# Both banks of a PSUM pair in turns for the early experts, an even pace for the threshold search, and a residual moved into the second attention

## The chip, the cores and the metric

The kernel runs on one core of a Trainium2 chip. The metric is the device time of one execution in microseconds (us). Times are the median of timed executions; beside them stands one execution taken with the hardware profiler, whose own time is given with its span.

## The reference

Sixteen batches of 256 tokens with 128 channels pass through four residual steps in fp32. The experts' step is used twice with the same weights.

```
x = x + attn_a(layernorm(x))      # 16 heads of 8 channels, sign-and-scale weights
x = x + ffn(layernorm(x))
x = x + attn_b(layernorm(x))      # 16 heads, with a table of relative positions
x = x + ffn(layernorm(x))

def ffn(x):                       # 8 experts of 512 hidden units, every token in every expert
    logits = einsum('bld,ed->ble', x, gate_weight)
    kth    = sort(logits.reshape(-1))[4 * 128 * 6 - 1]   # one threshold for all tokens
    gates  = logits * (logits >= kth)
    h      = gelu(einsum('bld,ehd->bleh', x, w1) + b1)
    y      = einsum('bleh,edh->blde', h, w2) + b2
    return einsum('blde,ble->bld', y, gates)
```

The threshold is one order statistic of all logits of the step. It is known only when the attention before it has finished its last batch, while the hidden layers of the experts need only the tokens of their own chunk.

## The kernel before

**Stages.** The order is the first attention, the first experts, the second attention, the second experts. A chunk is 512 tokens (two batches); there are 8 chunks (`NCHUNK`) and 8 experts (`NE`), so 64 pairs of chunk and expert per pass. For one pair `h_unit` (L1082) is one matmul of 128x512 into a PSUM tile `ph` and one gelu on ScalarE (ACT) into `hT`, four times; `y_unit` (L1093) is four matmuls of 128x512 into one tile `py`. One fp32 matmul is two records in the trace.

**Early experts.** The first two chunks (`EARLY` = 16 pairs of chunk and expert) do not wait for the threshold: `early` (L1102) is a generator that yields after each h unit and after each y unit, 80 pieces in all, and the y results go ungated to `raw` tiles by an ACT activation (L1116). Twenty pieces are taken at the end of the attention before (`own_at`, L1054, by the step `U` of the second attention: 20 pieces), the rest during the search.

**PSUM at the end of the second attention.** The scores of the second attention use three PSUM tiles with the tag `ss` of two banks each (L875). The early pieces there take tiles of the same tag through `bank` (L1074) and use the first bank of each, `[:, 0, :]`; a tile comes free for the next piece but two when ACT has read it. Two more banks have the tag `m`. All engines are written out by hand there (`manual_schedule`, L1009), so each queue runs in the order of the code: PE has, for steps `U` = 128 and on, the visits `first` and `second` of the last batches and between them the pieces.

**The search.** `search` (L1144) finds the threshold bit by bit in 11 counts. A count compares all logits with up to seven candidates on VectorE (DVE, lines L1137), sums over the partitions by a small matmul `pc` (L1141), and four small DVE operations choose the next candidates. `experts` (L1249) takes four early pieces for each of the 11 counts; where `pc` stands among them on PE is decided by the scheduler. After it the gates are turned by `pg` (L1259), written to DRAM, and read back as rows `gb` for each pair (L1189, seven buffers).

**The border from the first experts to the second attention.** The last pair of chunk and expert is done in halves of 256 tokens: `last_in_halves` (L1215) makes two `py` of four 128x256 matmuls each; each half is gated on DVE (L1225), added to the sum `acc` (L1228), transposed by two PE matmuls `f_pr` (L1236), and added to `x` (L1239). Then the second attention begins with its first matmuls L726 (queries of batch 1), whose PSUM bank belonged to the experts' pool, and the scores L884.

Of the kernel before, what the change touches and what calls it, by code (L numbers as in the profile page):

```python
# [10 lines left out]
F32 = mybir.dt.float32  # L11
I32 = mybir.dt.int32
AF = mybir.ActivationFunctionType
ALU = mybir.AluOpType
# [64 lines left out]
def hybrid_kernel(ctx: ExitStack, tc: tile.TileContext, io):  # L79
# [38 lines left out]
    def const(name):  # L118
        lo, hi = CONSTS[name]
        return head[:, lo:hi]  # L120
# [532 lines left out]
    def attention_b(outer):  # L653
# [35 lines left out]
        def values_tile(pool, i):  # L689

            va = pool.tile([P, NK, NJ, DH, NG], F32, tag=f"va{i}", name=f"b_va{i}")
            nc.gpsimd.memset(va, 0.0)
            vas.append(va)

        values_tile(wpool, 0)
        mask_h, mask_q = const("mask_h"), const("mask_q")
        NH2, NN = NH // 2, NQB // 2
        rows_of, xnTs, batch, vz, tall = {}, {}, {}, {}, {}
# [160 lines left out]
        def main(st, place, filling):  # L859
# [176 lines left out]
            def for_batch(f, b, *rest):  # L1036
# [13 lines left out]
                6: lambda b: for_batch(ahead_rows, b + 3),  # L1050
                7: lambda b: for_batch(ahead_spread, b + 1),
            }

            own_at = {0: 2, 1: 2, 2: 1, 4: 2, 5: 2, 6: 2, 8: 2, 9: 2, 10: 1, 12: 2, 13: 2}  # L1054
            done = 0
            for U in range(total + 2 * NU + 1):
                b, i = divmod(U, NU)
                table.get(i, lambda b: None)(b)
                if U < total:
                    scores(U)  # L1060
                while done < min(total, U - 1):
                    turn(done)
                    done += 1
                if U >= total:
                    place["h"] = (epool, 5, psum, "ss", 3)
                    place["y"] = (psum, "ss", 3)
                    place["raw"] = (epool, 4)
                    for _ in range(own_at.get(U - total, 0)):
                        own.append(next(filling))

        return begin, run


    def bank(psum, tag, name, bufs):  # L1074

        if callable(tag):
            return tag(name).rearrange("p t x -> p (t x)")
        if tag == "ss":
            return psum.tile([P, 2, CH], F32, tag=tag, name=name, bufs=bufs)[:, 0, :]
        return psum.tile([P, CH], F32, tag=tag, name=name, bufs=bufs)  # L1080

    def h_unit(place, c, e, k):  # L1082
# [37 lines left out]
                    yield  # L1120
            prev = (c, e, hs)

    def experts(last, place, raw, filling, middle):
        with ExitStack() as st:
            hpool = st.enter_context(tc.tile_pool(name="f_h", bufs=1))
            pool = st.enter_context(tc.tile_pool(name="f_2", bufs=2))
# [3 lines left out]

            def count(thresholds, name):

                n = len(thresholds)
                cnt = small.tile([P, NCAND], F32, tag="cnt", name=f"cnt{name}")
                for j, threshold in enumerate(thresholds):
                    ge = small.tile([P, NTILE * NE], F32, tag="ge", name=f"ge{name}_{j}", bufs=2)
                    nc.vector.tensor_scalar(  # L1137
                        ge, lf, threshold, 0.0, ALU.is_ge, ALU.add, accum_out=cnt[:, j : j + 1]
                    )
                pc = psum.tile([P, NCAND], F32, tag="c", name=f"pc{name}")  # L1140
                nc.tensor.matmul(pc[:, 0:n], ones, cnt[:, 0:n], start=True, stop=True)  # L1141
                return pc

            def search():  # L1144

                digits = const("digits")

                pc = count((0.0, 2.0, -2.0 + 2.0**-23), "s")  # L1150
                ok = small.tile([P, 3], F32, tag="ok_s", name="ok_s")
                held = small.tile([P, 1], F32, tag="held", name="held_s")
                nc.vector.tensor_scalar(
                    ok, pc[:, 0:3], NEED, 0.0, ALU.is_ge, ALU.add, accum_out=held
                )
                below = small.tile([P, 1], I32, tag="d", name="below")
                nc.vector.tensor_scalar(below, held, 2.0, -1.0, ALU.is_lt, ALU.mult)
                f = below
                for odd in (1.0, 3.0):
                    d = small.tile([P, 1], I32, tag="d", name=f"d_s{odd:.0f}")  # L1160
                    nc.vector.tensor_scalar(
                        d, held, odd, float(1 << 30), ALU.is_equal, ALU.mult
                    )
                    new = small.tile([P, 1], I32, tag="f", name=f"f_s{odd:.0f}")
                    nc.vector.tensor_tensor(new, f, d, ALU.bitwise_xor)
                    f = new
                yield
                for i in range(len(SHIFTS)):
                    at = slice(NCAND * i, NCAND * i + NCAND)
                    cand = small.tile([P, NCAND], I32, tag="cand", name=f"cand{i}")  # L1170
                    nc.vector.tensor_tensor(  # L1171
                        cand, flips[:, at], f.to_broadcast([P, NCAND]), ALU.bitwise_xor
                    )
                    values = cand.bitcast(F32)
                    pc = count([values[:, j : j + 1] for j in range(NCAND)], i)
                    ok = small.tile([P, NCAND], F32, tag="ok", name=f"ok{i}")
                    nc.vector.scalar_tensor_tensor(  # L1177
                        ok, pc, NEED, digits[:, at], ALU.is_ge, ALU.mult
                    )
                    d = small.tile([P, 1], I32, tag="d", name=f"d{i}")  # L1180
                    nc.vector.tensor_reduce(d, ok, AX.X, ALU.max)  # L1181
                    new = small.tile([P, 1], I32, tag="f", name=f"f{i}")
                    nc.vector.tensor_tensor(new, f, d, ALU.bitwise_xor)  # L1183
                    f = new
                    yield
                kth.append(f)

            def broadcast_gates(c, e):
                gb = pool.tile([P, CH], F32, tag="gb", name=f"gb{c}_{e}", bufs=7)  # L1189
                nc.sync.dma_start(  # L1190
                    gb.rearrange("p (t k) -> p t k", k=P),
                    gd[c * 4 * NE : (c + 1) * 4 * NE, :]
                    .rearrange("(t e) k -> e t k", e=NE)[e]
                    .partition_broadcast(P),
                )
                return gb
# [3 lines left out]
            def gated(c, e, y, bias):  # L1200

                gb = broadcast_gates(c, e)
                if e == 0:
                    accs[c] = pool.tile([P, CH], F32, tag="acc", name=f"acc{c}", bufs=2)
                    dst = accs[c]
                else:
                    dst = pool.tile([P, CH], F32, tag="gy", name=f"gy{c}_{e}")
                if bias is None:
                    nc.vector.tensor_tensor(dst, y, gb, ALU.mult)
                else:  # L1210
                    nc.vector.scalar_tensor_tensor(dst, y, bias, gb, ALU.add, ALU.mult)  # L1211
                if e:
                    nc.vector.tensor_tensor(accs[c], accs[c], dst, ALU.add)
# [32 lines left out]
            place["h"] = (hpool, 14, psum, "h", 3)  # L1246
            place["y"] = (psum, "y", 2)
            place["raw"] = (pool, EARLY - 4)
            for i, _ in enumerate(search()):  # L1249
                for _ in range(4):  # L1250
                    next(filling, None)
            gates = small.tile([P, NTILE * NE], F32, tag="ge", name="gates", bufs=2)
            nc.vector.scalar_tensor_tensor(
                gates, lf, kth[0].bitcast(F32), lf, ALU.is_ge, ALU.mult
# [13 lines left out]
            for i in range(EARLY, total + 1):  # L1268
                c, e = divmod(i, NE)
                hs, now, ready = None, ready, []  # L1270
                if i < total:
                    hs = [h_unit(place, c, e, k) for k in range(NHC)]
                if middle is not None and i >= total - 12 and i % 2 == 0:
                    next(middle(psum), None)
                if due < EARLY:
                    gated(*divmod(due, NE), raw[due], None)
                    due += 1
                    if due % NE == 0:
                        ready.append(due // NE - 1)
                if i == total:  # L1280
                    last_in_halves(*prev)
                elif prev is not None:
                    gated(
                        prev[0], prev[1], y_unit(place, *prev),
                        b2[:, prev[1] : prev[1] + 1],
                    )
                    if prev[1] == NE - 1:
                        ready.append(prev[0])
                for done in now:
                    residual(done)  # L1290
                prev = (c, e, hs)
            for done in ready:
                residual(done)

    epool = ctx.enter_context(tc.tile_pool(name="epool", bufs=1))
# [6 lines left out]
    ahead = fill()  # L1302
    attention_a(*ahead[::2])
    with ExitStack() as st:
        begin, run = attention_b(st)
        experts(False, *ahead, begin)
        ahead = fill()
        run(*ahead[::2])
    experts(True, *ahead, None)


def _spread(v, extra):
# [73 lines left out]
```

## Time and profile before

| | |
|---|---|
| timed runs | 1535.77, 1535.91 and 1536.73 us, median 1535.91 |
| profiled execution, own time | 1538.61 us |
| its span, first to last instruction | 1536.6 us |
| granted TensorE clock over the span | 0.999 |
| PE busy | 1523.6 us (99%), 12292 matmul records |
| ACT, DVE, POOL busy | 839.5, 799.5 and 406.4 us |
| second attention | about 740 to 1079 us of the span |
| early pieces at its end | 1078.8 to 1108.7 us |
| second search, from its first to its last `pc` | 1110.9 to 1168.3 us |

Times in views of the trace are microseconds from the start of the span. The row of a group gives busy time, mean duration and the idle time of its engine before it, with what ended that idle time. PE matmuls are pipelined and their ends are modelled, so the start of one record against the start of the next tells more of PE than the length of one.

### The profile page before, as it was taken

What the parts mean: (1) busy time and instruction counts of PE and PEld (TensorE: products, weight loads), DVE (VectorE), ACT (ScalarE), POOL (GpSimd) and SP (SyncE); (2) the same over time, 40 slices, a digit from 0 to 9 for tenths busy, and PEclk for the clock granted to TensorE, in tenths of its full rate; (3) what the DMA queues carried; (4) which work ended last, traced back from release to release, by engine and by line L of the source; (5) the groups of instructions that cost most, each with busy time, mean ns of one, the idle gap of its engine ahead of it and who ended that gap; (6) DMA issues with size and microseconds to landing.
All of it is one profiled execution on the core that took longest, in us unless ns stands there. A gap on an engine that the chain in (4) does not pass through costs nothing. (4 is left out here: it accounts for less than half of the span.)

```text
span 1536.6 us, 30874 instructions
## 1 busy us (share of the span) xinstructions
PE 1523.6 (99%) x12292; PEld 858.9 (56%) x12292; DVE 799.5 (52%) x1624; ACT 839.5 (55%) x2092; POOL 406.4 (26%) x521
## 2 busy tenths in 40 slices
PE   9999999999999999999999999999999999999998
PEld 6777777544444444444677777777444444444444
DVE  7878887254134221212699999999353143212222
ACT  4666666644434343434688888888544433434342
POOL 6323421200001000002488988886100000000000
PEclk9999999999999999999999999999999999999999
DMA  4511110000223211120122222221002133111110
GB/s 107 149 30 36 37 29 16 5 4 9 71 75 78 53 37 39 38 46 20 27 53 58 50 51 48 54 57 37 8 1 63 43 81 85 50 46 39 44 41 7
DMA packets 174127, 69.91 MB, mean 45 GB/s; under 512 B 74520, under 2 KB 173600, under 8 KB 173728
## 3 DMA queue, kind: packets, MB, share of 16 engines
q1 hardware_dynamic: 173408, 67.54, 18.7%
q8 instruction: 97, 1.59, 0.4%
q10 hardware_dynamic: 576, 0.41, 0.1%
q14 instruction: 46, 0.38, 0.1%
HBM read 50.88 MB, written 12.58 MB: 41 GB/s over the span
## 5 line engine op out<-in xcount | busy, mean ns | idle before, releaser
L1088 ACT ACTIVATE hT<-ph,head 128x512 f32<-128x512 f32 x512 | 351.1, 687 | 419.2 <-PE ph L1086 416.7
L1086 PE MATMUL ph<-xn,w 128*128 128x512 f32 x1024 | 464.3, 594 | 1.1 <-ACT hT L1088 1.1
L1097 PE MATMUL py<-hT,w 128*128 128x512 f32 (+1 forms) x1040 | 461.1, 586 | 1.0 <-ACT logits L985 0.5
L1097 PEld LDWEIGHTS py<-hT,w 128*128 128x128 f32 x1040 | 196.6, 190 | 237.3 <-issue 230.5
L1086 PEld LDWEIGHTS ph<-xn,w 128*128 128x128 f32 x1024 | 191.4, 190 | 228.5 <-issue 224.7
L1211 DVE SCALAR_TENSOR_TENSOR gy<-py,head,gb 128x512 f32<-128x512 f32 x82 | 61.5, 750 | 425.7 <-PE py L1097 425.7
L899 ACT ACTIVATE b_pr<-b_s,b_nm 128x256 f32<-128x256 f32 x512 | 235.9, 473 | 61.2 <-DVE b_nm L894 60.9
L455 DVE TENSOR_REDUCE a_nm<-a_s 128x2 f32<-128x512 f32 x256 | 158.5, 682 | 50.7 <-PE a_t L478 49.0
L894 DVE TENSOR_REDUCE b_nm<-b_s 128x4 f32<-128x1024 f32 x128 | 152.7, 1193 | 23.8 <-PE b_s L884 23.6
L884 PE MATMUL b_s<-b_kT,b_qd 64*64 64x256 f32 x1024 | 160.8, 384 | 0.0
L884 PE MATMUL b_s<-strip,b_qb 64*64 64x256 f32 x2048 | 157.6, 378 | 0.0
L884 PE MATMUL b_s<-b_kS,b_qd 64*64 64x256 f32 x1024 | 157.4, 384 | 0.0
L909 DVE STREAM_TRANSPOSE b_pT<-b_pr 128x1024 f32<-128x1024 f32 x128 | 157.1, 1228 | 0.0
L484 ACT ACTIVATE a_pT<-a_t 128x512 f32<-128x512 f32 x256 | 132.6, 602 | 29.2 <-PE a_t L478 28.8
L478 PE MATMUL a_t<-a_qa,a_qk 32*128 32x256 f32 x1024 | 133.8, 392 | 0.1
L774 POOL TENSOR_TENSOR b_qd<-b_qsel,head 128x512 f32<-128x512 f32 x64 | 84.1, 1335 | 179.8 <-DMA b_qsel<-b_qT 169.5
L450 PE MATMUL a_s<-a_qk 32*128 32x256 f32 x1024 | 128.4, 389 | 0.3 <-ACT a_qkc L416 0.3
L153 POOL TENSOR_SCALAR ve<-mv 128x2 f32<-128x2 f32 x64 | 14.8, 231 | 423.4 <-DVE mv L150 413.6
L450 PEld LDWEIGHTS a_s<-a_qk 32*128 32x128 f32 x1024 | 91.6, 184 | 22.6 <-issue 14.9
L899 ACT ACTIVATION_READ_ACCUMULATOR b_pr<-b_s,b_nm 128x1 f32 x512 | 104.1, 203 | 0.0
L478 PEld LDWEIGHTS a_t<-a_qa,a_qk 32*128 32x128 f32 x1024 | 99.7, 184 | 3.9 <-PE a_t L478 0.8
L162 POOL TENSOR_SCALAR xn<-x,mv,rstd 128x128 f32<-128x128 f32 x126 | 99.9, 803 | 6.6
(175 smaller groups left out, 1432.8 us busy)
## 6 DMA issues: line engine op xcount, KB each, us to landing
gb<-gd SPq DMA_DIRECT2D x128, 256.0 KB
w<-in_w SPq DMA_DIRECT2D x2, 2048.0 KB
a_qks<-a_qkc SPq DMA_DIRECT2D x15, 256.0 KB
a_qk<-a_qks SPq DMA_DIRECT2D x60, 64.0 KB
x<-in_x SPq DMA_DIRECT2D x16, 128.0 KB
b_qs<-b_qT SPq DMA_DIRECT2D x64, 32.0 KB
b_qsel<-b_qT SPq DMA_DIRECT2D x64, 32.0 KB
b_z<-b_qs SPq DMA_DIRECT2D x16, 128.0 KB
```

The source lines that it names most:

```text
L162: (last or nc.gpsimd).tensor_scalar(xn[:, t, :], xs[b][:, t, :], mv[:, t, 0:1], rstd[:, t : t + 1], ALU.subtract, ALU.mult,)
L450: nc.tensor.matmul(sc[:, t, :], q[b][rows, g, t * P : (t + 1) * P], k[b][rows, g, :], start=True, stop=True,)
L455: nc.vector.tensor_reduce(nms[G % 4][:, :, j, 0:1].rearrange("p t o -> p (t o)"), sc, AX.X, ALU.max, negate=True,)
L478: nc.tensor.matmul(sc[:, t, :], k[b][rows, g, t * P : (t + 1) * P], qaug[G][rows, :], start=True, stop=True,)
L484: nc.scalar.activation(pT, sc, AF.Exp)
L884: nc.tensor.matmul(sc[64 * c : 64 * c + 64, r, u, :], (qb_[rows, at, c] if rel else qd[rows, at, x]).rearrange("p h q -> p (h q)"), strip[ ...
L894: nc.vector.tensor_reduce(nm, sc, AX.X, ALU.max, negate=True)
L899: nc.scalar.activation(pr[:, u, r, :], sc[:, r, u, :], AF.Exp, bias=nm[:, r, u : u + 1], scale=1.0, accum_out=sums[b][:, n : n + 1],)
L909: nc.vector.transpose(pT[:, half % 2, 4 * i : 4 * i + 4].rearrange("p n k h q -> p (n k h q)"), probs.pop(U).rearrange("p u r k -> p (u r ...
L1086: nc.tensor.matmul(ph, w1[:, m * P : (m + 1) * P], xn2[c], start=True, stop=True)
L1088: nc.scalar.activation(hT, ph, AF.Gelu_apprx_tanh, bias=b1[:, m : m + 1], scale=1.0)
L1097: nc.tensor.matmul(py[:, 0:width], w2[:, e * NHC + k, :], hs[k], start=k == 0, stop=k == NHC - 1)
```

## The change

It has three parts. At the end of the second attention `bank` hands out both banks of an `ss` tile in turns, first bank and then second bank, before it takes a new tile. In the search the small matmul of a count stands after five early pieces, in an order on PE that is written by hand, and the yield stands between the comparisons and that matmul. For the first experts the last pair is no longer done in halves: its sum goes to a tile `late` in the attention's pool, and the transposes and the additions to `x` of chunk 7 are done by `add_late` in step `U` = 2 of the second attention. To make room `gb` has six buffers instead of seven in the first experts.

```diff
+        late = wpool.tile([P, CH], F32, tag="late", name="b_late_sum")
...
+            def add_late():
+                pr = psum.tile([P, 2 * T], F32, tag="m", name="b_late", bufs=2)
+                for t in range(4):
+                    nc.tensor.transpose(
+                        pr[:, t * P : (t + 1) * P], late[:, t * P : (t + 1) * P], ident
+                    )
+                for j in range(2):
+                    b = NB - 2 + j
+                    nc.vector.tensor_tensor(
+                        xs[b], xs[b],
+                        pr[:, j * T : (j + 1) * T].rearrange("p (t c) -> p t c", c=C), ALU.add,
+                    )
...
                 table.get(i, lambda b: None)(b)
+                if U == 2:
+                    add_late()
                 if U < total:
                     scores(U)
...
+    halves = []
     def bank(psum, tag, name, bufs):
...
         if tag == "ss":
-            return psum.tile([P, 2, CH], F32, tag=tag, name=name, bufs=bufs)[:, 0, :]
+            if not halves:
+                t = psum.tile([P, 2, CH], F32, tag=tag, name=name, bufs=bufs)
+                halves.extend((t[:, 1, :], t[:, 0, :]))
+            return halves.pop()
...
             def count(thresholds, name):
...
                         ge, lf, threshold, 0.0, ALU.is_ge, ALU.add, accum_out=cnt[:, j : j + 1]
                     )
+                yield
                 pc = psum.tile([P, NCAND], F32, tag="c", name=f"pc{name}")
...
-                    pc = count([values[:, j : j + 1] for j in range(NCAND)], i)
+                    pc = yield from count([values[:, j : j + 1] for j in range(NCAND)], i)
...
-                    yield
                 kth.append(f)
...
-                gb = pool.tile([P, CH], F32, tag="gb", name=f"gb{c}_{e}", bufs=7)
+                gb = pool.tile([P, CH], F32, tag="gb", name=f"gb{c}_{e}", bufs=7 if last else 6)
...
                 if e == 0:
-                    accs[c] = pool.tile([P, CH], F32, tag="acc", name=f"acc{c}", bufs=2)
+                    if c == NCHUNK - 1 and not last:
+                        accs[c] = late
+                    else:
+                        accs[c] = pool.tile([P, CH], F32, tag="acc", name=f"acc{c}", bufs=2)
...
-            for i, _ in enumerate(search()):
-                for _ in range(4):
-                    next(filling, None)
+            with tc.manual_schedule(engines={mybir.EngineType.PE}):
+                for _ in search():
+                    for _ in range(5):
+                        next(filling, None)
...
-                if i == total:
+                if i == total and last:
                     last_in_halves(*prev)
...
-            for done in ready:
+            for done in ready if last else ():
                 residual(done)
```

More of the change, by code (lines that the diff above doesn't have):

```diff
@@ L1069, in main @@
                         own.append(next(filling))
-        return begin, run
+        return begin, run, late
+    halves = []
     def bank(psum, tag, name, bufs):
@@ L1121, in early, with experts @@
             prev = (c, e, hs)
-    def experts(last, place, raw, filling, middle):
+    def experts(last, place, raw, filling, middle, late):
         with ExitStack() as st:
@@ L1148, in search @@
                 digits = const("digits")
-                pc = count((0.0, 2.0, -2.0 + 2.0**-23), "s")
+                pc = yield from count((0.0, 2.0, -2.0 + 2.0**-23), "s")
                 ok = small.tile([P, 3], F32, tag="ok_s", name="ok_s")
@@ L1184, in search @@
                     f = new
-                    yield
                 kth.append(f)
             def broadcast_gates(c, e):
-                gb = pool.tile([P, CH], F32, tag="gb", name=f"gb{c}_{e}", bufs=7)
+                gb = pool.tile([P, CH], F32, tag="gb", name=f"gb{c}_{e}", bufs=7 if last else 6)
                 nc.sync.dma_start(
@@ L1304, in hybrid_kernel @@
     with ExitStack() as st:
-        begin, run = attention_b(st)
-        experts(False, *ahead, begin)
+        begin, run, late = attention_b(st)
+        experts(False, *ahead, begin, late)
         ahead = fill()
         run(*ahead[::2])
-    experts(True, *ahead, None)
+    experts(True, *ahead, None, None)
 def _spread(v, extra):
```

## The prediction

> **What bounds the kernel now.** I read the engine totals first, then what PE waits for, then the timeline at the three places that the diff touches, and the busy time by windows beside them. In the totals
>
> ```profile
> PE 1523.6 (99%) x12292; PEld 858.9 (56%) x12292; DVE 799.5 (52%) x1624; ACT 839.5 (55%) x2092; POOL 406.4 (26%) x521
> ```
>
> PE is the bound, and the next engine has nearly half of the span to spare. A change that adds no matmuls can gain only what PE now waits, and loses what it makes PE wait. The list of PE's waits (total us, times, longest) says how little there is to gain:
>
> ```profile
> PE f_pr L1236 <- DVE acc L1228: 2.2, 2, 1.1
> ...
> PE ph L1086 <- ACT hT L1088: 1.1, 1, 1.1
> PE pc L1141 <- DVE ge L1137: 0.9, 4, 0.2
> ...
> PE b_m L726 <- DVE x L1239: 0.6, 1, 0.6
> ```
>
> All four belong to the three parts of the diff: border (first and last), second attention's end, search. Together they are 4.8 us.
>
> **Both banks in turns: what it does to the waits.** The diff reads as if six banks replaced three. The program built from the changed kernel says otherwise. Its semaphores guard the tile, not the bank: in each of the ten pairs the matmul into the second bank waits for ACT's read of the first (`ph0_0_1` for `hT0_0_0`, `ph0_0_3` for `hT0_0_2`, `py0_0` for `hT0_1_0`, and so on to `ph0_4_0` for `hT0_3_3`). Before, a piece waited only for the reader three tiles back. Only the early pieces at the second attention's end take this path; those of the first attention get their tiles from a function.
>
> What one such wait costs: PE's records of a 128x512 matmul start 0.429 us apart, two to a matmul, 0.86 us. The timelines of PE and of ACT (start, busy time, work, and in brackets the idle time before it and its cause) show
>
> ```profile
> 1078.81 3.04 PE L1086 MATMUL ph<-xn,w 128*128 128x512 f32 x6
> 1082.95 1.98 PE L1086 MATMUL ph<-xn,w 128*128 128x512 f32 x4 [1.10 <-ACT hT L1088]
> ```
>
> ```profile
> 1080.92 1.28 ACT L1088 ACT_TABLE_LOAD   x1
> 1082.21 2.59 ACT L1088 ACTIVATE hT<-ph,head 128x512 f32<-128x512 f32 x4
> 1084.97 0.69 ACT L1088 ACTIVATE hT<-ph,head 128x512 f32<-128x512 f32 x1 [0.17 <-PE ph L1086]
> ```
>
> ACT begins 0.20 after the last column, reads for 0.69, PE goes on 0.05 after its end, and the first record after a wait has 0.53 instead of 0.43. A bare wait is 0.20 + 0.69 + 0.05 + 0.10 = 1.04 us.
>
> Ten pairs: (1) `ph0_0_1` could start at 1079.67, but ACT's first gelu comes behind the table load and ends at 1082.90, so PE stands until 1082.95: 3.28 + 0.10. (3) two matmuls of values, 2.16 us, lie between the halves: 0. (6) gate and projection, 0.89, lie between: 0.1. The other seven halves follow each other directly: 7 x 1.04 = 7.3. The excess of the starts between 1078.81 and 1083.5 today, 1.67 us (1.27 of it the 1.10 wait), goes. Net +3.38 + 0.1 + 7.3 - 1.67 = **+9.1 us**. Nothing takes it back later, since PE has no gap there:
>
> ```profile
> 1079.00:1082.40 3.40, 2.82 (x6) 0.68 (x5) 3.37 (x9) 3.37 (x12) 1.29 (x3) 1.00 0.00 0
> 1086.00:1108.00 22.00, 22.00 (x91) 10.75 (x81) 1.12 (x5) 10.01 (x17) 3.38 (x5) 1.00 0.03 6
> ```
>
> (In these rows: window, its length, busy time of PE, PEld, DVE, ACT and POOL, PE's clock, DMA.)
>
> **The clock.** At the border the granted clock halves for one stretch of 3.4 us, right after a stretch in which PE was busy for half:
>
> ```profile
> 737.60:741.00 3.40, 1.71 (x12) 0.93 (x10) 1.56 (x4) 0.00 (x0) 0.95 (x1) 1.00 0.02 5
> 741.10:744.50 3.40, 3.40 (x36) 2.13 (x36) 0.00 (x0) 2.22 (x3) 0.00 (x0) 0.50 0.19 20
> ```
>
> About 1 us of idle time near 1081 did not do that. The new 3.3 us stop will probably cost one such stretch: 3.4 us at half speed lose 1.7; I take 1.2, bounds 0 and 1.7, and more if the seven waits that follow, one in each 2 to 3 us, keep the clock down.
>
> The Trainium skill ("TensorE: Matmul & The Clock Gate", Part 1) lets the clock fall only after a whole idle window of about 3.4 us; the row above fell after a window that was half busy, so by the row the new stop is enough, and by the page it is at the edge and the sum would be 1.2 less.
>
> **The search.** Today the second search shows
>
> ```profile
> 1135.06 0.28 PE L1141 MATMUL pc<-cnt,ones 128*128 128x7 f32 x2
> 1135.20 3.68 PE L1086 MATMUL ph<-xn,w 128*128 128x512 f32 x8
> 1139.11 0.39 PE L1141 MATMUL pc<-cnt,ones 128*128 128x7 f32 x2 [0.23 <-DVE ge L1137]
> ```
>
> With four matmuls between two `pc`, DVE's chain (four small steps and seven compares, about 3.9 us) is just longer than PE's work. Four such places, at 342, 371, 1138 and 1167 us, each lose 0.40 on the matmul's last record and 0.10 on `pc` (records 0.83 instead of 0.43, 0.13 instead of 0.03): 2.0. Longer `pc` starts in the rest of the searches add 0.4. With a `pc` after every five pieces, about eight matmuls or 6.9 us by the built order, the 3.9 us chain is done each time: **-2.4 us**. The end of the search, and so the gates, is about 19 matmuls later (16 us). That is covered: the first `gb` lands 7.9 us after `pg`, while the first tile whose release needs a `gb` is reached 21 matmuls (18 us) after it. `pg` itself has 1.9 us of matmuls ahead and needs 1.5. If the cover failed, the overhang of some 2 us would show as a wait of `py`.
>
> **The border.** Today, on PE,
>
> ```profile
> 737.40 0.38 PE L1236 MATMUL f_pr<-head,acc 128*128 128x128 f32 x2
> 738.90 0.41 PE L1236 MATMUL f_pr<-head,acc 128*128 128x128 f32 x2 [1.11 <-DVE acc L1228]
> 739.89 1.13 PE L726 MATMUL b_m<-b_xnT,b_w 128*128 128x256 f32 x4 [0.58 <-DVE x L1239]
> ```
>
> From the last column of `py7_71` to `b_m` are 2.49 us, of which 0.44 are transposes. In the changed order `b_m` waits only until DVE has multiplied the whole last `py` (512 wide): 0.20 + 0.75 + 0.10 = 1.05. The transposes come back in `U` = 2, at 0.44 plus 0.2 for the change of shape. 2.49 - 1.05 - 0.64 = **-0.8 us**. The half clock behind it has its cause removed: -1.7 in the profiled execution. That execution is 2.7 us above the median (1538.61 against 1535.91), and its span alone, 1536.6, is 0.7 above it, so timed runs may not always pay this; for them I take half, **-0.85**.
>
> **At nothing, with the cover.** Six `gb` instead of seven: one is used per pair, 6.9 us, and the load needs 7.9, so two would do; without the cover a late one costs its overhang each time. The last three `gb` rows of chunk 7 go behind four loads of the second attention on SP, and the last is issued near 700 for use at 737. The two additions to `x` (0.42 each on DVE) stand before the visit's own DVE work in `U` = 2 as they stood before it at the border; DVE is free half of the time. If PE waited for them it would be 0.8. `b_late` takes a bank of tag `m`, whose next user waits for those additions: the same 0.8. PE's waits for POOL near 791 (about 1.3 us) may move either way by as much.
>
> **Sums.** Profiled: 9.1 + 1.2 - 2.4 - 0.8 - 1.7 = +5.4, own time 1538.6 + 5.4 = 1544.0. Timed: 1535.9 + 9.1 + 1.2 - 2.4 - 0.8 - 0.85 = **1542.2 us**.
>
> **Rivals.** *The banks do work apart* (faster). If the second half does not in fact wait for ACT, all three parts gain: 1535.9 - 1.67 - 2.4 - 0.8 - 0.85 = 1530.2. For it speaks that ACT reads one bank while PE writes another throughout the attention. Against it stand the waits in the built program, which PE must obey. The outcome turns faster once the pairs cost less than 5.7 us gross, that is, less than the table-load wait and two bare waits. Chance 0.06.
>
> The Trainium skill ("PSUM — Partial Sum Buffer", section "PSUM bank collisions raise a hardware error") calls two engines on different banks clean; by that rule the halves need no wait and the sum would be the 1530 above, but what the chip permits does not take out a wait that the program holds.
>
> *It cancels.* If ACT's read begins sooner than I think after each matmul, or half of the halves have other work between, the pairs cost 5 us and the result is within 3 us of today, 0.2%, about what a measurement here can tell from no change. The window row 1086 to 1108, with PE at 22.00 of 22.00, and the order of the built program are against it. Chance 0.05.
>
> *The clock stays down.* Eight stops within 30 us could keep the clock at half for three to six stretches of 3.4 us, 1.7 each: 3 to 9 more, 1546 to 1551. The row at 741 is for it; against it, none of the bare waits leaves PE idle for even a third of such a stretch. Chance 0.08.
>
> **The numbers.** Forecast 0.81. Its own bounds: pairs +-1, clock -1.2 to +0.5, border clock +-0.85, search +-0.5, waits at POOL +-1.3; not all at once, 1539.0 to 1545.5. To leave out no more than 2 in 10 I go from 1538.8, where most cancelling cases end, to 1546.5 into the low end of the clock's case. Faster 0.06, same 0.05, slower 0.89.
>
> **What would show it.** In the changed profile: a wait of `ph` for `hT` near 1080 of about 3 us, and about seven of `ph` or `py` for `hT` or `raw` of 0.9 between 1083 and 1118; a half clock near 1083 and none at 741; no wait of `pc`; `b_m` about 1.1 after the last `py`. I am wrong if PE shows no such waits in the pairs, if the gates come late (`py` waiting behind `gb`), or if the seven waits are half as long.

## The result, and the profile after

The changed kernel takes 1543.49 us (median of 1543.03 to 1544.57) against 1536.32 before (the three runs above and one more of 1536.95), a ratio of 1.0045 with a 95% interval of 1.0033 to 1.0056: 7.2 us slower, where 6.3 were forecast. Its profiled execution has an own time of 1543.03 and a span of 1541.2, that is 4.4 and 4.6 us over those of before, where the forecast for this pair was 5.4.

The engine totals show no new work, and PE still at 99%:

```profile
PE 1523.1 (99%) x12284; PEld 856.1 (56%) x12284; DVE 799.5 (52%) x1622; ACT 840.0 (54%) x2092; POOL 406.2 (26%) x521
```

The list of what PE waits for (total us, times, longest) tells where the time went. The wait of `pc` and one of the two waits of `f_pr` are gone; the wait of `ph` for `hT` has grown from 1.1 to 8.9 us in eight places, seven short and one of 3.1:

```profile
PE ph L1110 <- ACT hT L1112: 8.1, 7, 3.1
...
PE f_pr L1264 <- DVE acc L1256: 1.1, 1, 1.1
PE b_m L728 <- DVE gy L1239: 0.8, 1, 0.8
PE ph L1121 <- ACT hT L1112: 0.8, 1, 0.8
```

(A matmul into the second bank appears under the tile's name, so a `py` is listed as `ph` where a `ph` has the first bank.) PE's timeline at the second attention's end has the long wait first, then the short ones one after another:

```profile
1073.74 1.02 PE L1110 MATMUL ph<-xn,w 128*128 128x512 f32 x2
...
1077.88 3.43 PE L1110 MATMUL ph<-xn,w 128*128 128x512 f32 x4 [3.12 <-ACT hT L1112]
1082.09 1.98 PE L1110 MATMUL ph<-xn,w 128*128 128x512 f32 x4 [0.78 <-ACT hT L1112]
...
1091.46 1.98 PE L1110 MATMUL ph<-xn,w 128*128 128x512 f32 x4 [0.84 <-ACT hT L1112]
1094.28 1.12 PE L1110 MATMUL ph<-xn,w 128*128 128x512 f32 x2 [0.84 <-ACT hT L1112]
```

The two matmuls (four records) after the long wait take 3.43 us instead of 1.98. The windows (length, busy time of PE, PEld, DVE, ACT and POOL, PE's granted clock, DMA) say why: after a window in which PE stood still for most of the time, the next one ran at half clock.

```profile
1074.00:1077.40 3.40, 0.76 (x2) 0.00 (x0) 3.37 (x9) 3.37 (x12) 1.36 (x3) 1.00 0.00 0
1077.41:1080.81 3.40, 2.93 (x4) 1.17 (x4) 0.82 (x1) 1.11 (x2) 1.85 (x3) 0.50 0.31 43
```

At the border `b_m` starts 1.43 us after the start of the last `py` record, 1.00 after its columns are through, and the transposes come later between the scores. No half clock follows:

```profile
735.49 0.59 PE L1121 MATMUL py<-hT,w 128*128 128x512 f32 x1
736.92 1.13 PE L728 MATMUL b_m<-b_xnT,b_w 128*128 128x256 f32 x4 [0.84 <-DVE gy L1239]
...
741.60 0.66 PE L1059 MATMUL b_late<-head,b_late_sum 128*128 128x128 f32 x4
```

```profile
735.50:738.90 3.40, 2.56 (x23) 1.35 (x25) 1.44 (x2) 0.76 (x2) 0.95 (x1) 1.00 0.02 5
738.90:742.30 3.40, 3.40 (x60) 2.22 (x56) 1.79 (x2) 2.42 (x7) 0.00 (x0) 1.00 0.30 31
```

In the search PE runs through; `pc` has no bracket behind it:

```profile
1147.56 3.60 PE L1110 MATMUL ph<-xn,w 128*128 128x512 f32 x8
1151.00 0.28 PE L1168 MATMUL pc<-cnt,ones 128*128 128x7 f32 x2
1151.14 3.68 PE L1121 MATMUL py<-hT,w 128*128 128x512 f32 x8
```

Setting the two traces side by side by PE's own milestones: the changed kernel is 5.07 us ahead when the last score of the second attention starts, and 4.64 behind at the first `f_pr` after the second search. In between it lost 9.71 us net of what the second search gained there.

### The profile page after: what moved, and what is told of

Read it like the earlier page. It is cut to its first block, busy times and chain, and to the rows that moved or that the text cites. A ratio compares the mean times of both kernels' runs of the same rounds, so it can differ in the third digit from the quotient of the medians.

```text
span 1541.2 us, 30857 instructions
## 1 busy us (share of the span) xinstructions
PE 1523.1 (99%) x12284; PEld 856.1 (56%) x12284; DVE 799.5 (52%) x1622; ACT 840.0 (54%) x2092; POOL 406.2 (26%) x521
## 5 line engine op out<-in xcount | busy, mean ns | idle before, releaser
L1121 PE MATMUL py<-hT,w 128*128 128x512 f32 (+1 forms) x1016 | 455.2, 591 | 1.0 <-ACT logits L987 0.5
L1121 PEld LDWEIGHTS py<-hT,w 128*128 128x128 f32 x1016 | 190.7, 190 | 226.4 <-issue 220.0
```

Source lines behind the costliest of these rows:

```text
L1121: nc.tensor.matmul(py[:, 0:width], w2[:, e * NHC + k, :], hs[k], start=k == 0, stop=k == NHC - 1)
```

## The experiments

The theory is that the framework's semaphores order write, read, write within a tile, whichever bank is meant, so adjacent halves make PE wait for ACT, while search and border gain. There are three rivals: the loss comes in part from late gates or the moved transposes; second banks as such are slow; the half clock has a cause other than PE standing still.

### Each part alone

The second attention's pairs alone: the kernel before with only this edit.

```diff
-            return psum.tile([P, 2, CH], F32, tag=tag, name=name, bufs=bufs)[:, 0, :]
+            if not halves:
+                t = psum.tile([P, 2, CH], F32, tag=tag, name=name, bufs=bufs)
+                halves.extend((t[:, 1, :], t[:, 0, :]))
+            return halves.pop()
```

> The kernel before with only the bank hand-out changed (both banks of an ss tile in turns). Theory, the second half waits for ACT's read of the first: seven bare waits of 1.10 us, 3.4 at the first pair, 1.4 for half clock behind it, less the 1.67 us of waits there today: +10.5 to +11.2 us against before, with seven or eight waits of ph for hT in the list of PE's waits and one 3.4 us stretch at clock 0.50. Rival, the loss of the changed kernel comes partly from late gates or from the border: pairs alone cost under 8 us.

Measured: 1548.61 us, ratio 1.0073 (1.0061 to 1.0086), +12.3 us. All of the loss is in the pairs, and more than expected. The waits are those of the changed kernel; the clock differs. In this profiled execution it stayed at half for three windows, 10.24 us:

```profile
1075.50:1078.90 3.40, 1.19 (x5) 0.36 (x4) 3.37 (x8) 3.29 (x11) 0.95 (x2) 1.00 0.00 0
1078.91:1082.31 3.40, 2.50 (x3) 1.17 (x4) 1.25 (x2) 1.23 (x3) 2.27 (x3) 0.50 0.26 39
1082.32:1085.72 3.40, 2.62 (x4) 0.84 (x3) 0.00 (x0) 0.97 (x2) 0.00 (x0) 0.50 0.13 39
1085.73:1089.13 3.40, 3.40 (x23) 1.33 (x25) 0.00 (x0) 1.37 (x2) 0.00 (x0) 0.50 0.00 0
```

Its timed runs fall in two groups by the granted clock of the span: 1546.4 and 1546.7 at 0.999, and 1548.6 to 1549.0 at 0.997 and 0.998. This fits a cost that depends on how many windows the clock stays down; only the one profiled execution shows the windows themselves.

The changed kernel without the pairs (the edit above taken back):

> The changed kernel with one bank per tile at the second attention's end, as before; search and border stay changed. Theory: faster than before by the search (2.5 us) and the border (0.8 to 1.3 us, and up to 1.7 more if the kernel before pays a half clock at the border in its timed runs too): 3.3 to 6 us under before; no wait of pc, no half clock at the border. Rival, late gates or the moved transposes give the gain back: within 2 us of before.

Measured: 1532.28 us, 0.9972 (0.9961 to 0.9983), 4.1 us under before, as the theory has it. Against it the changed kernel's pairs cost 11.2 us. The wait of `ph` at the table load is back at its old size, that of `pc` is gone, and nothing waits for `gb`:

```profile
PE f_pr L1260 <- DVE acc L1252: 1.1, 1, 1.1
PE ph L1106 <- ACT hT L1108: 1.1, 1, 1.1
PE b_m L728 <- DVE gy L1235: 0.8, 1, 0.8
```

The search alone, on the kernel before:

```diff
+                yield
                 pc = psum.tile([P, NCAND], F32, tag="c", name=f"pc{name}")
...
-            for i, _ in enumerate(search()):
-                for _ in range(4):
-                    next(filling, None)
+            with tc.manual_schedule(engines={mybir.EngineType.PE}):
+                for _ in search():
+                    for _ in range(5):
+                        next(filling, None)
```

> The kernel before with only the search changed (small matmul after five pieces, order of PE by hand). Theory: -2.0 to -2.8 us, no waits of pc for ge, no new wait of py for gb. Rival, gates 16 us later stall the gated pairs: 0 or slower, with waits of py that lead to gb.

Measured: 1534.77 us, 0.9986 (0.9977 to 0.9995), -1.6 us in the times. In the traces the first search gains 1.1 (from the last `a_mx`, the first attention's last matmul, to the last `py`) and the second 1.3 (from the first early `ph` to the first `f_pr`), 2.3 together before rounding. No wait of `py` leads to `gb`.

The border alone (late sum, `add_late`, six `gb`; the old search and single banks):

> The kernel before with only the border changed (last pair not in halves, residual of chunk 7 in U = 2, six gb in the first experts). Theory: -0.8 to -1.3 us if timed runs of before do not pay the half clock at the border, -2.5 to -3 if they do; b_m within 1.5 us after the start of the last py record, no stretch at clock 0.50 near 740. Rival, the transposes and additions in U = 2 hold up the scores: 0 or slower, with a wait near 742.

Measured: 1534.56 us, 0.9987 (0.9978 to 0.9996), -1.8 us. This lies between the two values expected, and the timed runs suggest why. Of 31 runs of the kernel before that stand beside the first seven experiments, 17 lie at 1535.0 to 1536.6 and 14 at 1536.9 to 1538.9; the granted clock is 1.000 in 12 of the 17, and 0.999 or less in all of the 14. (In nine more, beside the last two experiments, two of 1536.8 and 1537.4 have 1.000, so the split is not clean.) The kernel with the border changed has one level, 1534.0 to 1534.8. This fits a half clock at the border in about half of the executions of before, which the new border ends; the profiled execution of before, with its stretch at 741, is one with it.

One trace shows an execution without it. The profile of the pairs alone has the border of before, and there the window from 737.58 to 740.99, with 1.82 us of PE work, is followed by full clock. From the first `b_m` to the last score of the second attention, the same code in both, it takes 332.8 us where the profile of before takes 335.6.

### Which order makes the wait

Three tiles open at once, first banks of all three, then second banks:

```diff
             if not halves:
-                t = psum.tile([P, 2, CH], F32, tag=tag, name=name, bufs=bufs)
-                halves.extend((t[:, 1, :], t[:, 0, :]))
+                ts = [
+                    psum.tile([P, 2, CH], F32, tag=tag, name=f"{name}_{j}", bufs=bufs)
+                    for j in range(3)
+                ]
+                halves.extend(t[:, n, :] for n in (1, 0) for t in reversed(ts))
```

> The changed kernel, but three ss tiles are open at once and handed out as first banks of all three, then second banks of all three. Both banks are used as much as in the changed kernel, only the second bank's write is three pieces behind the first's. Theory, the cost is the wait of one piece for the reader of the piece just before it in the same tile: the seven waits are gone, and the time is that of the changed kernel without pairs, 9.5 to 11.5 us under the changed kernel, 3 to 6 under before. Rival, writing second banks as such is slow (a conflict of PE and ACT in one tile): 3 us or more above that.

Measured: 1532.25 us, 0.9969 (0.9956 to 0.9981), equal to the kernel without pairs (1532.28). Both banks are written as often as in the changed kernel and the 11 us are gone. It is not the second bank that costs, but writing it right behind the first.

The first piece in a tile of its own, pairs from the second piece on:

```diff
                 t = psum.tile([P, 2, CH], F32, tag=tag, name=name, bufs=bufs)
+                if not began:
+                    began.append(name)
+                    return t[:, 0, :]
                 halves.extend((t[:, 1, :], t[:, 0, :]))
```

> The changed kernel, but the first early piece takes a tile of its own, and the pairs begin with the second piece. Theory: the 3.1 us stop behind the table load and the half clock behind it change, the short waits of 0.84 stay, some at other pieces. The second piece then needs no read; the third piece (second bank) waits for the gelu of the second, which lies behind the table load and the first gelu, from 1.0 us of PE later: a stop of some 3 us stays, and the half clock with it, so the time is within 2 us of the changed kernel. Rival, only a stop that begins with the table load itself halves the clock: 1.4 us or more faster and no stretch at 0.50.

Measured: 1543.49 us, 1.0040 (1.0026 to 1.0054), the same as the changed kernel. The stop only moved to the third piece, 2.8 us:

```profile
1078.90 1.98 PE L1113 MATMUL ph<-xn,w 128*128 128x512 f32 x4 [2.84 <-ACT hT L1115]
```

But its profiled execution shows no half clock, which neither side had expected. Here the stop lies across the border of two windows (the borders are 3.413 us apart, read back from the clock's record at the end of the run):

```profile
1074.58:1077.98 3.40, 1.48 (x4) 0.38 (x2) 3.37 (x9) 3.37 (x11) 1.50 (x3) 1.00 0.00 0
1077.99:1081.39 3.40, 1.98 (x4) 0.68 (x4) 0.68 (x1) 2.01 (x4) 1.72 (x3) 1.00 0.32 48
```

So this run alone doesn't separate its two theories; three of its five timed runs have a clock of 0.998 and are over 1 us longer than the other two, as if the stretch were there in some executions.

Two matmuls of a group first, then their two reads, on top of the changed search and border:

```diff
-        nc.scalar.activation(
+        read(lambda: nc.scalar.activation(
             hT, ph, AF.Gelu_apprx_tanh, bias=b1[:, m : m + 1], scale=1.0
-        )
+        ))
...
+                    pair["on"], pair["tile"], pair["reads"] = n == 2, None, []
                     for _ in range(n):
                         own.append(next(filling))
+                    pair["on"] = False
+                    for f in pair["reads"]:
+                        f()
```

`read` keeps the ACT instruction back while `pair["on"]` holds, and `bank` gives the group's two pieces the two banks of one tile.

> The changed search and border, and both banks of a tile in use at the second attention's end, but the two matmuls of a group of two pieces are issued before the two reads by ACT, so that the second half's matmul stands ahead of the first half's reader in the program and waits for no reader of its own tile. Theory, the wait comes from the order write, read, write in one tile: no wait of ph for hT near 1080 at all, not even today's 1.1 us, 0.8 to 1.8 us faster than the changed kernel without pairs, 4 to 8 under before. Rival, ACT now starts each first read 0.86 us later and falls behind, so PE waits at the y units instead: as fast as the kernel without pairs or slower, with waits of py for hT.

Measured: 1531.47 us, 0.9963 (0.9951 to 0.9976), 0.8 under the kernel without pairs. With the same two banks and the same two matmuls in a row, but the reads behind both, PE waits for no `hT` there; even the 1.1 us that the kernel before waits at the table load are gone. PE runs ten records (five matmuls) without a stop. It lost part of the gain at one place, where its wait for the copy of the logits grew from 0.5 to 1.13 us; on ACT that copy now stands behind two gelus:

```profile
1074.42 4.46 PE L1122 MATMUL ph<-xn,w 128*128 128x512 f32 x10
...
1104.49 3.70 PE L1133 MATMUL py<-hT,w 128*128 128x512 f32 x8 [1.13 <-ACT logits L987]
```

The same for the first two groups only (`U - total < 2` in place of `n == 2`):

> As the kernel that issues two matmuls before their two reads, but only for the first two groups of early pieces; the other pieces take one bank of a tile each. Theory, the gain lies at the table load alone, and the longer wait of py for logits near 1104 (1.1 instead of 0.5 us) came from two gelus that stood before the copy of the logits: that wait is 0.5 again, no wait of ph for hT, and the time is 0.3 to 0.8 us under that kernel, near 1530.8. Rival, the later pairs gain as well: equal or slower than it.

Measured: 1530.71 us, 0.9961 (0.9948 to 0.9975), as expected. The wait for the logits is 0.5 again. This version beats both kernels: 6.1 us under the 1536.83 of before that was run beside it, and 12.8 under the changed kernel's 1543.49.

```profile
1073.68 4.46 PE L1122 MATMUL ph<-xn,w 128*128 128x512 f32 x10
1078.22 1.95 PE L920 MATMUL b_m<-b_pT,b_va 128*32 128x128 f32 x64
```

### The clock

The changed kernel with work in the long stop:

```diff
                         own.append(next(filling))
+                        if len(own) == 1:
+                            fill = psum.tile([P, 2 * T], F32, tag="m", name="b_fill", bufs=2)
+                            for _ in range(3):
+                                nc.tensor.matmul(
+                                    fill, w1[:, 0:P], xn2[0], start=True, stop=True
+                                )
```

> The changed kernel with three more matmuls of 128x512 (2.6 us of PE, into a spare bank that nobody reads) between the first and the second early piece, where PE otherwise stands for 3.1 us. They add no time to the chain there, since the second piece still waits for the first gelu. Theory, the half clock follows from PE standing still: no stretch at 0.50 near 1077, the wait of ph there falls from 3.1 to about 0.5 us, and the time is 1.4 us (one stretch) to 3 us under the changed kernel, 1540.5 to 1542. Rival, the clock falls for another reason, or the short waits alone bring it down: 1543 to 1544 and the stretch stays.

Measured: 1541.96 us, 1.0037 (1.0025 to 1.0050), 1.5 under the changed kernel, with 2.6 us of PE work added. The wait falls from 3.12 to 0.54, the window of the stop is nearly full, and the next keeps its clock:

```profile
1077.81 1.98 PE L1116 MATMUL ph<-xn,w 128*128 128x512 f32 x4 [0.54 <-ACT hT L1118]
```

```profile
1074.00:1077.40 3.40, 3.27 (x8) 1.14 (x6) 3.37 (x9) 3.37 (x12) 1.43 (x3) 1.00 0.00 0
1077.40:1080.80 3.40, 2.21 (x5) 0.90 (x6) 0.76 (x1) 1.74 (x3) 1.80 (x3) 1.00 0.27 43
```

The border between the two windows lies 3.8 us after the first early piece, against 3.7 in the changed kernel's profile, so the grid is not the difference. From the first early piece to the first `f_pr` after the search PE takes 186.6 us instead of 188.1. So in the changed kernel's profiled execution it was PE standing still that made the half clock. The 1.5 us in the times go the same way, but the two ratios' intervals overlap. Two of its five timed runs, at 1543.1 and 1544.5, have a clock of 0.999 against 1.000 of the other three (1541.5 to 1542.0); where those lost it, these runs don't show.

## Why the prediction was right

**The pairs** were the step that decided, and it held piece by piece. One stop of 3 us and seven short waits stood where the forecast put them: pairs 1, 2, 4, 5, 7, 8, 9 and 10, and none at 3 and 6. (What lies between the halves of pair 3 is 64 records of values and a transpose, not two matmuls; its 2.16 us are right.) A bare wait costs 1.10 us, by starts of records (1.43 and 0.53 instead of 0.43 each), against 1.04 in the sum; ACT begins 0.26 after the last column, not 0.20. In the trace the pairs cost 9.6 without the clock (9.71 net, plus the 1.3 of the second search, less 1.4 of half clock), against 9.1.

**The clock** was sized at 1.2 and was 1.4 in the profiled execution (1.01, 0.85, 0.85 and 1.49 instead of 0.53, 0.43, 0.43 and 1.43). That the stretch would come was a judgement, not a reading: a stop of 2.8 us in the profile of the first piece alone had none. The rival in which the clock stays down, held unlikely, is real for some executions: three windows in the profile of the pairs alone. With the clock the pairs cost 11.0 in the trace and 11.2 in the times against 10.3 forecast, and the 0.9 in the times is what the result lies above the forecast. In the trace 0.5 of the excess are waits and 0.2 are clock; how it divides in the timed executions is not shown.

**Search and border** together made -4.1 in the times, forecast -4.05. That is closer than the interval of about 1.7 either way lets one claim. The parts alone gave -1.6 and -1.8, with intervals of about 1.4 either way, so the times do not settle their own sizes. In the traces the search gains 2.3 against 2.4 forecast.

**The half clock at the border** was rightly counted in part, for the gap between the profiled execution and the median; that the part is a half was a guess that the two levels of before then bore out. It may have a second price that the sum had only as a bound: the medians of the two levels are 2.3 us apart, not 1.7. In the traces with the stretch (before, and the search alone) PE also waits some 1 us for POOL near 791; in the other traces this wait is shorter or absent, and it is absent in that of the pairs alone, whose code is the same up to there. Whether the stretch causes it was not tried. These waits are also why the profiled execution rose by less than forecast: they gave back 1.1 us and the stages before the first search 0.4, while the pairs took 0.7 more.

**The cover** of the edits costed at nothing held: no wait of PE for `gb`, for `pg` or for the additions of `add_late` in the changed profile. The second search ended 19.3 us later, not the 16 of the forecast: in the profile of the search alone its last `pc` starts 108.8 us after the first early piece, against 89.5 before.

**The rivals.** That the banks work apart is out as the kernel stands. It is half right: with the reads behind both matmuls they do, and then all three parts gain, at 1530.7 where the rival said 1530.2. The PSUM page that the prediction named ("PSUM — Partial Sum Buffer" of the Trainium skill, section "PSUM bank collisions raise a hardware error") agrees with these runs: in the profile with the first two groups only, ACT reads the first bank from 1077.08 to 1077.77 while PE writes another from 1077.11 on, and PE waits for no `hT` there. That it cancels is out: the pairs cost 11.2 us, not 5.

## What to carry to other kernels

Splitting a two-bank tile into halves doesn't give two buffers if the second write stands right behind the first half's reader in the program: look up what the built program waits for, and put both writes ahead of both reads, or let other tiles come between. On an engine that is 99% busy, count every new wait in full, and for a stop of some microseconds add the half clock that may follow. An execution's granted clock to three places is only a hint whether it did: in the profile with both matmuls first, the last 1.6 us of the span alone, at half clock, make it 0.999. When one profiled execution lies above the median of the runs, look for a stretch of half clock before its waits are counted as gain.

## What the runs showed of the hardware

The half clock comes in windows of 3.413 us on a fixed grid: before the last matmuls, the stretches in the clock's record last 3.413 or 10.240 us, and the stretches of full clock between two of them are whole multiples of 3.413. Where the grid falls differs from execution to execution; its first border lies between 0.05 and 2.99 us after the start of the span in the eleven profiles. It followed windows with PE busy for 0.76 and 1.19 us of 3.40 at the second attention's end and 1.71 at the border of before; it did not follow 1.82 at the same border in the profile of the pairs alone, nor 1.48 and 1.98 at a stop of nearly the same length split by the grid. Busy time alone is thus no exact criterion (part of the 1.71 are transposes; whether these count is open). Once down, the clock stayed down behind windows with 2.50 and 2.62 busy, and came back behind 2.93 and 3.40, while at full clock windows with 2.16 and 2.62 did not bring it down.

"TensorE: Matmul & The Clock Gate" of the Trainium skill (Part 1) has the clock fall after at least one idle window of about 3.4 us. The window's length agrees with the 3.413 here. Read as a window without any work, the rule does not hold: 1.19 and 1.71 us of work in it were not enough to keep the clock up.
